# A residual block with conditional rows in fp32 on one core: another order of the first products, and half of the row-block loads issued by ScalarE

## The chip, the core and the metric

One core of a Trainium2 chip runs the kernel. The metric is device microseconds (us) of the program, from its start to its end, as the median of several executions. The hardware profile comes from one execution.

## The reference

The output is `x + relu(concat(x, mean(x), cond, cond) · W + b)` in fp32, with x of four batch rows by 1024 by 512. Cut to what is computed:

```
hidden   = concat([cond, cond], -1)                       # (4, 512)
x_mean   = mean(x, axis=1, keepdims=True)
fused    = concat([x, x_mean, hidden], -1)                # last axis 1536
relation = relu(einsum('bld,do->blo', fused, W) + b)      # W is (1536, 512)
out      = x + relation
```

Only the first 512 rows of W meet every row of x. The mean and the condition give one vector of 512 per batch row, which the kernel works out once for each and adds as a bias.

## The kernel before, in words

**The products.** x has 4096 rows, cut into 32 tiles t of 128 rows. The 512 inputs of a row are cut into four chunks j. TensorE multiplies in a rounded fp32 form, so both sides are split: hi is the rounded value and lo what is left. For each tile and chunk there are three products, `product(t, j, n)` (L356): n=0 is hi·w_hi, n=1 is lo·w_hi, n=2 is hi·w_lo. That is 32·4·3 = 384 matmuls of 128x512 (L366), twelve of them adding up in one PSUM bank per tile. A task `p8.1` is the three products of tile 8 and chunk 1, and `p0.3.2` is a single one.

**How x gets to TensorE.** TensorE needs x transposed, with the inputs on the partitions. Tiles 0 to 3 come row by row (`X`, L206), are gathered (`y`, L232: a copy into another order) and transposed by TensorE itself (`T`, L261, into the PSUM tiles px, po and acc). From tile 4 on, a unit of four tiles comes as a z tile, in four quarters: `Zu.i` (L177) loads partitions 32i to 32i+31 of the z tile of unit u, 256 KB each in pieces of 512 bytes. There are three z buffers, and units 3 to 9 make 28 quarters. VectorE then transposes a chunk of the unit with a stream transpose (`T`, L263) into px or xT. Each transpose is read twice: ScalarE rounds it to hi and sums it for the mean (`h`, L270), and VectorE or GpSimd subtracts hi to get lo (`l`, L276). The weights come the same way: `W` (L181) loads a chunk, `wh` (L215) makes w_hi and `wl` (L222) makes w_lo.

**The rest.** `M` loads four chunks of the mean's weights, `V` the condition's weights (1 MB), `C` and `B` the condition and b. The tasks ac, t, g, d, to, as, m, f, fa, vh, vl, pb and bc work out the bias of each batch row. `K`, `b`, `r`, `F` and `S` take a finished tile out of its bank, add the bias, clamp it, add x and store it.

**What sets the order.** There is no scheduler. The table `ORDER` (L22 to L50) names the tasks one after another, and the loop at L457 issues them as they stand. Letters behind `@` choose an engine: d is VectorE, a is ScalarE, p is GpSimd. Each engine works through its own instructions strictly in that order. A `dma()` (L147) marked `@a` is issued by ScalarE and all others by SyncE (SP), each engine with its own queue. So `W0@a` and `W1@a` are the only transfers that ScalarE issues before the change. `fill` (L133) is a matmul on zeros ahead of the work.

**Semaphores of the transfers.** The transfers take eight semaphores, DMAHW0 to DMAHW7, in turn, whichever engine issues them. A transfer whose semaphore was used eight transfers earlier is issued only when that earlier one has landed. The engine that issues it stands still until then. In the order rows below, that is what `[waits DMAHW2_49]` behind a DMA says.

Of the kernel before, what the change touches and what calls it, by code (L numbers as in the profile page):

```python
# [19 lines left out]


ORDER = """  # L22
W0@a fill W1@a X0.0 X0.1 W2 fill relu fill W3 fill X0.2 fill Z3.1 fill y0.1@d y0.0@p y0.2@p fill T0.0 wh0r@d Z3.2
T0.1 T0.2 wh0l@d h0.0 fill wl0r@p fill y1.0@d y1.1@a T0.3 l0.0@d fill h0.2 wl0l@p fill h0.1 T1.2 T1.0 p0.0.1 T1.1
wh1@d Z3.3 T1.3 p0.0.0 h1.0 p0.0.2 Z3.0 h1.3 l1.0@d p1.0.2 wl1@p h1.2 l0.1@d p1.0.0 l1.3@d wh2@a p0.1.0 p1.0.1 wh3@d
h1.1 p0.1.1 p0.2.0 h0.3 l0.2@d wl2@p C p1.2.0 l1.1@d p1.3.1 V p0.3.0 p1.1.0 B y3.0@d y2.0@a p1.3.0 p0.2.1 Z4.0
l1.2@d p1.1.1 wl3@d p1.1.2 p0.2.2 T2.2 Z4.2 T2.3 p1.2.1 h2.2 T2.0 T2.1 l2.2@d p0.3.2 Z4.3 h2.0 p1.2.2 p3.2 h2.3
l2.0@d h2.1 l2.3@d p2.0 l2.1@d Z4.1 l0.3@d p2.3 p2.2 T3.0 p3.1 T3.3 h3.0 T3.1 p3.0 h3.3 l3.0@d p2.1 h3.1 l3.3@p t3
p3.3 T3.2 M1 K2@d p1.3.2 l3.1@p M0 p0.3.1 K1@a p4.0 t2 M2 h3.2 p0.1.2 ac0@p p6.0 M3 l3.2@d K0@a p4.3 Z5.2 t0 K3@d
p5.3 t1 Z5.3 ac1@d g0.0 p7.2 p6.2 d0.0 Z5.0 g0.1 p5.2 d0.1 g1.0 p5.0 Z5.1 T4.1 T4.3 p5.1 d1.0 T4.2 p6.3 K5@a Z6.0  # L30
T4.0 as0 p4.2 to0 g1.1 p7.3 Z6.3 h4.1 m0.0 p6.1 g2.0 l4.1@p m0.1 p4.1 Z6.2 h4.2 m0.2 p7.1 K4@a m0.3 h4.3 p7.0 Z6.1
K6@a p8.1 l4.3@p l4.2@d h4.0 X4.1 p10.1 f0 Z7.2 d1.1 p9.1 fa0 Z7.1 p10.3 l4.0@d vh0 d2.0 p8.2 g2.1 vl0 Z7.0 p11.2
K7@a T5.3 d2.1 p11.3 T5.2 h5.3 Z7.3 p8.0 T5.0 l5.3@p T5.1 pb0 p10.0 bc0@a h5.0 p10.2 b1@p h5.1 X1.1 l5.0@d p9.3 X2.0
h5.2 b2@d p9.0 as1 Z8.2 to1 p9.2 r1@a l5.1@p l5.2@d p12.3 r2@a X1.0 m1.0 K9@a p8.3 Z8.0 F1@p T6.3 p11.0 T6.1 h6.3
p12.2 b0@p m1.1 h6.1 p12.0 T6.2 K8@a p12.1 b3@p g3.0 T6.0 p11.1 K10@a m1.2 Z9.3 h6.2 d3.0 p13.1 Z8.3 m1.3 h6.0 p14.0
Z8.1 l6.0@d f1 b4@p p13.3 r0@a l6.2@d p14.1 r3@a T7.2 l6.3@p p15.0 fa1 Z9.2 p13.0 T7.0 vh1 F2@p p15.1 K11@a vl1 X5.0
p13.2 F0@d Z9.0 b6@p p15.2 S1 T7.3 pb1 X5.1 l6.1@p p14.3 bc1@a as2 p14.2 K13 F3@p r6@a p16.0 K12 h7.3 p15.3 K14 h7.2
l7.3@p T7.1 p17.0 b5@d h7.1 p19.3 b9@p h7.0 p17.3 r4@a l7.0@d p19.2 to2 g3.1 l7.2@d F4@p p16.2 r5@a m2.0 p18.3 K15
b8@p S4 p18.2 Z9.1 m2.1 p16.3 X3.1 d3.1 m2.2 p19.0 m2.3 p18.1 F5@p T8.0 p16.1 f2 fa2 p20.3 b11@p S5 T8.3 S2 p17.2
vh2 X3.0 h8.0 vl2 p17.1 F6@p X2.1 h8.3 S3 T8.2 p19.1 l7.1@d b7@p S6 p20.0 X4.0 pb2 S0 p18.0 bc2@a l8.3@p X7.0 h8.2  # L40
p20.2 K17 r7@a p20.1 K16 as3 F7@p p22.2 T8.1 l8.0@d p21.3 h8.1 T9.0 S7 r8@a p21.1 l8.1@p X6.1 K19 r11@a p22.1 r9@a
l8.2@d b10@p p22.0 r14@a K18 p21.2 r13@a T9.1 h9.0 p24.2 F13@p T9.2 h9.1 p24.1 T9.3 h9.2 F8@p F9@d p21.0 r15@a p24.0
r10@a F11@p S8 K20 h9.3 p22.3 S13 K21 r17@a p23.1 X6.0 to3 r21@a p23.0 F10@p m3.0 r18@a p23.3 r20@a m3.1 p26.1
l9.3@p m3.2 p25.0 K22 F21@p p23.2 m3.3 r22@a p26.2 F15@p f3 S21 p24.3 S11 r12@a fa3 p27.3 S10 F17@p K23 S15 vh3
p25.1 S9 r16@a vl3 p25.2 r19@a F16@p r23@d p26.0 l9.0@d p25.3 F19@p S16 pb3 X7.1 p26.3 bc3@a S17 F12@p P28 p27.1 K25
p27.2 l9.2@d P30 F18@p p28.2 F14@d r25@a p30.2 l9.1@p K26 p28.0 S14 S18 F25@d P31l p27.0 S19 F23@p r26@a p30.0 K24
S25 p31.2l F26@p S23 K27 p31.0l r24@a S12 p31.1l P29 p31.3l F20@p p30.3 P31r F31l F22@d S31l p29.1 S26 p28.1 S20
r27@d S22 p29.0 F24@d F27@p p28.3 p29.3 F28 S24 p30.1 S27 S28 p29.2 F30 p31.1r F29 S30 p31.0r p31.3r S29 p31.2r F31r
S31r
""".split()  # L50


# [437 lines left out]
```

## Time and profile before

| what | value |
|---|---|
| median of 3 runs | 102.18 us (102.05 to 102.19) |
| span of the profiled execution | 101.1 us |
| TensorE busy, of the span | 95.8 us (95%) |
| VectorE, ScalarE, GpSimd busy | 79.3, 60.6, 80.0 us |
| granted TensorE clock, mean of the core | 0.999 |
| moved by DMA | 27.36 MB, mean 271 GB/s |

The span runs from the first to the last instruction of the profiled execution. The time has about 1.1 us more, which lies around the span. A matmul of 128x512 is shown with 0.39 us though the next starts 0.23 us later, since matmuls are pipelined. In the rows a name such as `lo<-xT,hi` says what is written from what, with the buffers' numbers left out.

### The profile page before, as it was taken

The page shows a single profiled execution, that of the slowest core. Times are in us where ns is not written, and L with a number is a line of the kernel's source. Part 1 is how long each engine was busy: PE and PEld are TensorE (multiplying, and loading weights), DVE is VectorE, ACT ScalarE, POOL GpSimd, SP SyncE. Part 2 cuts the span into 40 slices and gives each one's busy share as a digit, 9 for nine tenths or more (in the row PEclk, how much of TensorE's full clock was granted, in tenths as well). Part 3 has the DMA queues.
Part 4 walks back from the last instruction along what each step waited for, and adds up shares of the span by engine and source line. Part 5 has one row for each costly group of instructions (what it writes and reads, how often), then busy time and mean ns, then how long its engine had stood idle before and what let it go on. Part 6 is the DMA issues. An engine that isn't in the chain of part 4 may idle for free.

```text
span 101.1 us, 1437 instructions
## 1 busy us (share of the span) xinstructions
PE 95.8 (95%) x427; PEld 76.4 (76%) x427; DVE 79.3 (78%) x129; ACT 60.6 (60%) x150; POOL 80.0 (79%) x77
## 2 busy tenths in 40 slices
...
GB/s 46 372 343 227 210 211 316 205 205 322 207 199 191 210 223 197 206 260 298 241 225 209 207 254 307 265 359 408 405 397 400 274 219 345 282 403 328 310 381 161
DMA packets 25345, 27.36 MB, mean 271 GB/s; under 512 B 1397, under 2 KB 15993, under 8 KB 25338
## 3 DMA queue, kind: packets, MB, share of 16 engines
...
q8 instruction: 3, 0.05, 0.2%
...
HBM read 18.88 MB, written 8.39 MB: 270 GB/s over the span
## 4 chain that ended last, share of the span: by engine, by line
PE 38%; DMA 23%; POOL 18%; DVE 10%; ACT 4%; issue 2%; ACTq 1%; SPq 1%; POOLq 0%
PE po L366 37%; DMA z<-in_x_dram 9%; POOL x L455 8%; DMA x<-in_x_dram 8%; DMA x<-in_L_cond_W_dram 6%; POOL lo L276 4%; POOL o L437 4%; DVE acc L320 2%; DVE lo L276 2%; ACT hi L270 2%; DVE w_hi L220 1%; DVE o L446 1%; POOL cond L302 1%; DVE o L441 1%; PE px L261 1%
## 5 line engine op out<-in xcount | busy, mean ns | idle before, releaser
L366 PE MATMUL po<-w_hi,lo 128*128 128x512 f32 (+1 forms) x132 | 50.7, 387 | 0.5 <-DVE lo L276 0.4
L366 PE MATMUL po<-w_hi,hi 128*128 128x512 f32 (+1 forms) x132 | 50.2, 385 | 0.0
L366 PE MATMUL po<-w_lo,hi 128*128 128x512 f32 (+1 forms) x132 | 50.1, 385 | 0.0
L455 POOL TENSOR_TENSOR x<-o,x 128x512 f32<-128x512 f32 x22 | 30.0, 1385 | 0.7 <-DVE o L446 0.4
L366 PEld LDWEIGHTS po<-w_hi,lo 128*128 128x128 f32 x132 | 24.8, 188 | 6.1 <-DVE lo L276 0.8
L366 PEld LDWEIGHTS po<-w_hi,hi 128*128 128x128 f32 x132 | 24.8, 188 | 5.4 <-DVE o L441 0.6
L366 PEld LDWEIGHTS po<-w_lo,hi 128*128 128x128 f32 x132 | 24.7, 188 | 5.0 <-ACT hi L270 0.3
L276 POOL TENSOR_TENSOR lo<-xT,hi 128x512 fp32r<-128x512 f32 x13 | 17.7, 1367 | 9.2 <-ACT hi L270 9.2
L448 ACT ACTIVATE o<-o 128x512 f32<-128x512 f32 x26 | 15.2, 622 | 4.0 <-DVE o L441 3.4
L437 POOL TENSOR_TENSOR o<-o,bias 128x512 f32<-128x512 f32 x10 | 13.9, 1390 | 0.0
L276 DVE TENSOR_TENSOR lo<-px,hi 128x512 fp32r<-128x512 f32 (+2 forms) x20 | 11.5, 588 | 2.2 <-ACT hi L270 2.2
L270 ACT ACTIVATE hi<-px 128x512 fp32r<-128x512 f32 (+2 forms) x20 | 10.3, 517 | 4.8 <-DVE px L263 2.5
L320 DVE SCALAR_TENSOR_TENSOR acc<-w_mean,tot,acc 128x512 f32<-128x512 f32 x16 | 12.0, 748 | 1.4 <-POOL tot L311 1.1
L441 DVE TENSOR_TENSOR o<-po,bias 128x512 f32<-128x512 f32 x16 | 10.5, 679 | 1.6 <-POOL x L455 1.4
L263 DVE STREAM_TRANSPOSE xT<-z 128x512 f32<-128x512 f32 x14 | 9.4, 687 | 2.2 <-POOL cond L302 2.2
L263 DVE STREAM_TRANSPOSE px<-z 128x512 f32<-128x512 f32 x14 | 9.5, 699 | 2.0 <-DMA z<-in_x_dram 1.8
L270 ACT ACTIVATE hi<-xT 128x512 fp32r<-128x512 f32 x14 | 8.7, 624 | 1.8 <-DVE xT L263 1.7
L455 DVE TENSOR_TENSOR x<-o,x 128x512 f32<-128x512 f32 x6 | 7.2, 1194 | 0.0
L298 ACT ACTIVATE term<-wc,cT 128x512 f32<-128x512 f32 x8 | 5.7, 718 | 2.2 <-DVE cT L284 1.4
L433 ACT ACTIVATE o<-po 128x512 f32<-128x512 f32 x10 | 5.9, 590 | 0.8 <-PE po L366 0.8
L302 POOL TENSOR_TENSOR cond<-b_sb,term 128x512 f32<-128x512 f32 x4 | 5.2, 1292 | 1.0 <-ACT term L298 1.0
L224 POOL TENSOR_TENSOR w_lo<-x,w_hi 128x256 fp32r<-128x256 f32 (+1 forms) x4 | 4.2, 1068 | 1.8 <-DVE w_hi L220 1.8
...
## 6 DMA issues: line engine op xcount, KB each, us to landing
out_dram<-x SPq DMA_DIRECT2D x31, 256.0 KB, 3.2
...
z<-in_x_dram SPq DMA_DIRECT2D x28, 256.0 KB, 9.6
x<-in_L_cond_W_dram SPq DMA_DIRECT2D x1, 1024.0 KB, 9.4
w_mean<-in_L_cond_W_dram SPq DMA_DIRECT2D x4, 256.0 KB, 8.2
x<-in_L_cond_W_dram ACTq DMA_DIRECT2D x2, 256.0 KB, 4.6
x<-in_x_dram SPq DMA_DIRECT2D x2, 256.0 KB, 2.8
x<-in_L_cond_W_dram SPq DMA_DIRECT2D x2, 256.0 KB, 5.5
```

The lines of the kernel that those rows point to most:

```text
L263: nc.vector.transpose(xT.rearrange("p (n q e) -> p n q e", q=Q // E, e=E), zs[z_of(u)][:, : n * NQ].rearrange("p n (q j e) -> p n j q e", ...
L270: nc.scalar.activation(his[buf][:, col : col + m], xT, AF.Copy, accum_out=sums[:, r, j, s : s + 1])
L276: nc_of[e].tensor_tensor(los[buf][:, col : col + m], xT, his[buf][:, col : col + m].bitcast(F32), ALU.subtract)
L298: nc.scalar.activation(terms[k], wc[:, k], AF.Copy, scale=cT[:, k, r : r + 1])
L302: nc.gpsimd.tensor_tensor(conds[r % 2], conds[r % 2] if k else b_sb, terms[k], ALU.add)
L320: nc.vector.scalar_tensor_tensor(acc, w_mean[:, j, :], tot[:, r, j : j + 1], acc, ALU.mult, ALU.add)
L366: nc.tensor.matmul(v, lhsT=a[:, col : col + P], rhs=m, start=WAYS[t] != "I" and key not in done, stop=done.count(key) == 3 * J - 1, skip_g ...
L433: nc.scalar.activation(o, bank(t), AF.Copy)
L437: nc_of[e].tensor_tensor(o, o, biases[r], ALU.add)
L441: nc.vector.tensor_tensor(o, bank(t), biases[r], ALU.add)
L448: nc.scalar.activation(o, o, AF.Relu)
L455: nc_of[e].tensor_tensor(x_tile(t), o, x_tile(t), ALU.add)
```

## The change

The code is the same but for the table `ORDER`, which has one line fewer, so every line number after it is smaller by one (L270 becomes L269). The table changes in two ways.

**The first eleven us.** Tile 0 is transposed chunk by chunk in the order 0 to 3, the first product is hi·w_hi (`p0.0.0`) and not lo·w_hi, and tiles 0 and 1 go on together, chunk by chunk. Chunk 3 of w_hi (`wh3`) is made by ScalarE and not by VectorE. All 24 products of tiles 0 and 1 stand before the first of tile 3 (`p3.2`); before, 21 did, and `p1.3.2`, `p0.3.1` and `p0.1.2` came later. Tiles 2 and 3 are transposed in two groups with other work between, not in one. There are 10 fills, not 11.

**The quarters.** Quarters 2 and 3 (partitions 64 to 127) of units 3 to 9 are issued by ScalarE (`@a`): 14 transfers. The quarters of a unit stand together in the order 0, 1, 2, 3. Before, all 28 were issued by SP, mostly spaced out and in orders such as 1, 2, 3, 0 or 0, 2, 3, 1.

The upper part of the diff; the rest of the table changes in the places of Z alone:

```diff
-W0@a fill W1@a X0.0 X0.1 W2 fill relu fill W3 fill X0.2 fill Z3.1 fill y0.1@d y0.0@p y0.2@p fill T0.0 wh0r@d Z3.2
-T0.1 T0.2 wh0l@d h0.0 fill wl0r@p fill y1.0@d y1.1@a T0.3 l0.0@d fill h0.2 wl0l@p fill h0.1 T1.2 T1.0 p0.0.1 T1.1
-wh1@d Z3.3 T1.3 p0.0.0 h1.0 p0.0.2 Z3.0 h1.3 l1.0@d p1.0.2 wl1@p h1.2 l0.1@d p1.0.0 l1.3@d wh2@a p0.1.0 p1.0.1 wh3@d
-h1.1 p0.1.1 p0.2.0 h0.3 l0.2@d wl2@p C p1.2.0 l1.1@d p1.3.1 V p0.3.0 p1.1.0 B y3.0@d y2.0@a p1.3.0 p0.2.1 Z4.0
-l1.2@d p1.1.1 wl3@d p1.1.2 p0.2.2 T2.2 Z4.2 T2.3 p1.2.1 h2.2 T2.0 T2.1 l2.2@d p0.3.2 Z4.3 h2.0 p1.2.2 p3.2 h2.3
-l2.0@d h2.1 l2.3@d p2.0 l2.1@d Z4.1 l0.3@d p2.3 p2.2 T3.0 p3.1 T3.3 h3.0 T3.1 p3.0 h3.3 l3.0@d p2.1 h3.1 l3.3@p t3
-p3.3 T3.2 M1 K2@d p1.3.2 l3.1@p M0 p0.3.1 K1@a p4.0 t2 M2 h3.2 p0.1.2 ac0@p p6.0 M3 l3.2@d K0@a p4.3 Z5.2 t0 K3@d
-p5.3 t1 Z5.3 ac1@d g0.0 p7.2 p6.2 d0.0 Z5.0 g0.1 p5.2 d0.1 g1.0 p5.0 Z5.1 T4.1 T4.3 p5.1 d1.0 T4.2 p6.3 K5@a Z6.0
-T4.0 as0 p4.2 to0 g1.1 p7.3 Z6.3 h4.1 m0.0 p6.1 g2.0 l4.1@p m0.1 p4.1 Z6.2 h4.2 m0.2 p7.1 K4@a m0.3 h4.3 p7.0 Z6.1
-K6@a p8.1 l4.3@p l4.2@d h4.0 X4.1 p10.1 f0 Z7.2 d1.1 p9.1 fa0 Z7.1 p10.3 l4.0@d vh0 d2.0 p8.2 g2.1 vl0 Z7.0 p11.2
-K7@a T5.3 d2.1 p11.3 T5.2 h5.3 Z7.3 p8.0 T5.0 l5.3@p T5.1 pb0 p10.0 bc0@a h5.0 p10.2 b1@p h5.1 X1.1 l5.0@d p9.3 X2.0
-h5.2 b2@d p9.0 as1 Z8.2 to1 p9.2 r1@a l5.1@p l5.2@d p12.3 r2@a X1.0 m1.0 K9@a p8.3 Z8.0 F1@p T6.3 p11.0 T6.1 h6.3
...
+W0@a fill W1@a X0.0 X0.1 W2 fill relu fill W3 fill X0.2 Z3.0 Z3.1 fill fill y0.0@d y0.1@a y0.2@p fill T0.0 T0.1 h0.0
+T0.2 T0.3 wh0r@d h0.1 wh0l@d p0.0.0 wl0r@p l0.0@d h0.2 wl0l@p y1.0@d y1.1@a p0.0.1 h0.3 l0.1@d fill T1.0 T1.1 fill
+T1.2 T1.3 p0.0.2 h1.0 l0.2@d h1.1 l0.3@d p1.0.0 h1.2 l1.0@d p1.0.2 h1.3 wh1@d p1.0.1 fill p0.1.0 wl1@p wh2@a l1.1@d
+p1.1.0 p0.1.1 l1.2@d wh3@a Z3.2@a Z3.3@a C V B Z4.0 Z4.1 p1.1.1 p0.2.0 l1.3@d wl2@d p1.2.0 p0.2.1 wl3@p p1.2.1 p0.1.2
+p1.1.2 p0.3.0 p1.3.0 p0.3.1 p1.3.1 y3.0@d y2.0@a p0.2.2 p1.2.2 T2.2 h2.2 T2.0 h2.0 l2.2@d l2.0@d p0.3.2 p1.3.2 T2.3
+h2.3 T2.1 h2.1 Z4.2@a Z4.3@a l2.3@d l2.1@d p3.2 p2.0 p2.3 p2.2 T3.0 p3.1 T3.3 h3.0 T3.1 p3.0 h3.3 l3.0@d p2.1 h3.1
+l3.3@p t3 p3.3 T3.2 M1 K2@d l3.1@p M0 K1@a p4.0 t2 M2 h3.2 ac0@p p6.0 M3 l3.2@d K0@a Z5.0 Z5.1 Z5.2@a Z5.3@a p4.3 t0
+K3@d p5.3 t1 ac1@d g0.0 p7.2 p6.2 d0.0 g0.1 p5.2 d0.1 g1.0 p5.0 T4.1 T4.3 p5.1 d1.0 T4.2 p6.3 Z6.0 Z6.1 Z6.2@a Z6.3@a
+K5@a T4.0 as0 p4.2 to0 g1.1 p7.3 h4.1 m0.0 p6.1 g2.0 l4.1@p m0.1 p4.1 h4.2 m0.2 p7.1 K4@a m0.3 h4.3 p7.0 K6@a p8.1
+l4.3@p l4.2@d h4.0 X4.1 p10.1 f0 Z7.0 Z7.1 Z7.2@a Z7.3@a d1.1 p9.1 fa0 p10.3 l4.0@d vh0 d2.0 p8.2 g2.1 vl0 p11.2 K7@a
+T5.3 d2.1 p11.3 T5.2 h5.3 p8.0 T5.0 l5.3@p T5.1 pb0 p10.0 bc0@a h5.0 p10.2 b1@p h5.1 X1.1 l5.0@d p9.3 X2.0 h5.2 b2@d
+p9.0 as1 to1 p9.2 r1@a l5.1@p l5.2@d p12.3 r2@a X1.0 m1.0 K9@a Z8.0 Z8.1 Z8.2@a Z8.3@a p8.3 F1@p T6.3 p11.0 T6.1 h6.3
...
```

ScalarE's own order around the loads of units 3 and 4. po, px and xT are what is transposed or evacuated, o_112 the gathered copy of tile 2 (`y2.0`), z_69 the z tile of unit 3 and z_70 that of unit 4. Before:

```order
L218 ACTIVATE w_hi<-x_63 128x512 [waits DMAHW4_49]
L270 ACTIVATE hi_76,sums<-acc 128x128 [waits DVE_49]
L270 ACTIVATE hi_75,sums<-po_140 128x128
L237 ACTIVATE o_112<-x_65 128x512 [waits DMAHW6_49]
L270 ACTIVATE hi_78,sums<-px_142 128x256 [waits PE_49]
L270 ACTIVATE hi_77,sums<-px_141 128x256 [waits PE_49]
L270 ACTIVATE hi_78,sums<-px_142 128x256 [waits DVE_49]
L270 ACTIVATE hi_77,sums<-px_141 128x256 [waits DVE_49]
L270 ACTIVATE hi_79,sums<-px_141 128x512 [waits DVE_49]
```

After:

```order
L217 ACTIVATE w_hi<-x_63 128x512 [waits DMAHW5_49]
L147 DMA z_69<-in_x_dram 32x16x128
L147 DMA z_69<-in_x_dram 32x16x128 [waits DMAHW6_49]
L236 ACTIVATE o_112<-x_65 128x512
L269 ACTIVATE hi_78,sums<-px_142 128x256 [waits PE_49]
L269 ACTIVATE hi_77,sums<-px_141 128x256 [waits PE_49]
L269 ACTIVATE hi_78,sums<-px_142 128x256 [waits DVE_49,PE_49]
L269 ACTIVATE hi_77,sums<-px_141 128x256 [waits DVE_49,PE_49]
L147 DMA z_70<-in_x_dram 32x16x128 [waits DMAHW2_49]
L147 DMA z_70<-in_x_dram 32x16x128 [waits DMAHW6_49]
L269 ACTIVATE hi_79,sums<-px_141 128x512 [waits DVE_49]
```

Four transfers now stand in ScalarE's stream, two ahead of the gathered copy of tile 2 and two ahead of hi_79, the first hi of unit 3. DMAHW6 is the last load of the first rows (`X0.2`) for the first of these waits and Z3.3 for the second. DMAHW2 is `V`.

ScalarE's order around the loads of unit 6 (z_69 again), ahead of hi_84, the first hi of unit 4. Before:

```order
L298 ACTIVATE term_122<-wc,cT 128x512 [waits Pool_49]
L433 ACTIVATE o_108<-po_136 128x512 [waits PE_49]
L315 ACTIVATE acc<-cond_124 128x512 [waits Pool_49]
L298 ACTIVATE term_123<-wc,cT 128x512 [waits Activation_49]
L270 ACTIVATE hi_84,sums<-xT_120 128x512 [waits DVE_49]
```

After, with the two loads ahead of o_108:

```order
L297 ACTIVATE term_122<-wc,cT 128x512 [waits Pool_49]
L147 DMA z_69<-in_x_dram 32x16x128 [waits DMAHW6_49]
L147 DMA z_69<-in_x_dram 32x16x128 [waits DMAHW0_49]
L432 ACTIVATE o_108<-po_136 128x512 [waits PE_49]
L314 ACTIVATE acc<-cond_124 128x512 [waits Pool_49]
L297 ACTIVATE term_123<-wc,cT 128x512 [waits Activation_49]
L269 ACTIVATE hi_84,sums<-xT_120 128x512 [waits DVE_49]
```

ScalarE now passes two loads before it can evacuate o_108 and come to hi_84. SP's order after the change, from the loads of unit 5 (z_71) to those of unit 6 (z_69):

```order
L147 DMA z_71<-in_x_dram 32x16x128 [waits DMAHW5_49]
L147 DMA z_71<-in_x_dram 32x16x128 [waits DMAHW7_49]
L147 DMA z_69<-in_x_dram 32x16x128 [waits DMAHW0_49,DVE_49]
L147 DMA z_69<-in_x_dram 32x16x128 [waits DMAHW2_49]
L147 DMA x_63<-in_x_dram 128x2x512 [waits DMAHW4_49,Pool_49]
```

ScalarE's DMA row that waits for DMAHW0 is Z6.3, and the transfer that used DMAHW0 last is Z6.0, the third of SP's rows. ScalarE comes to Z6.3 only after `Z6.2`, and goes on to o_108 only after Z6.3.

TensorE's order around the transposes of tiles 2 and 3 (o_112 and o_111 into px). Before:

```order
L261 MATMUL px_142<-term_123,o_112 128x128 [waits Activation_49]
L261 MATMUL px_142<-term_123,o_111 128x128 [waits DVE_49]
L261 MATMUL px_142<-term_123,o_112 128x128
L261 MATMUL px_142<-term_123,o_111 128x128
L366 MATMUL po_137<-w_hi,lo_90 128x512 [waits DVE_49]
L261 MATMUL px_141<-term_123,o_112 128x128
L261 MATMUL px_141<-term_123,o_111 128x128
L261 MATMUL px_141<-term_123,o_112 128x128
L261 MATMUL px_141<-term_123,o_111 128x128
L366 MATMUL po_136<-w_lo,hi_75 128x512 [waits DVE_49]
L366 MATMUL po_137<-w_lo,hi_76 128x512
L366 MATMUL po_139<-w_hi,hi_78 128x512 [waits Activation_49]
```

After:

```order
L260 MATMUL px_142<-term_123,o_112 128x128 [waits Activation_49]
L260 MATMUL px_142<-term_123,o_111 128x128 [waits DVE_49]
L260 MATMUL px_141<-term_123,o_112 128x128
L260 MATMUL px_141<-term_123,o_111 128x128
L365 MATMUL po_136<-w_lo,hi_75 128x512 [waits Pool_49]
L365 MATMUL po_137<-w_lo,hi_76 128x512
L260 MATMUL px_142<-term_123,o_112 128x128 [waits DVE_49]
L260 MATMUL px_142<-term_123,o_111 128x128
L260 MATMUL px_141<-term_123,o_112 128x128 [waits DVE_49]
L260 MATMUL px_141<-term_123,o_111 128x128
L365 MATMUL po_139<-w_hi,hi_78 128x512 [waits Activation_49]
```

The second group of four transposes now waits for VectorE, twice: it writes into px beside what l2.2 and l2.0 still read, and stands ahead of the first product of tile 3 (po_139).

## Rows read from the trace of the kernel before

**Rows 1.** The page: the span

```profile
span 101.1 us, 1437 instructions
```

**Rows 2.** Windows: us, busy PE, PEld, DVE, ACT, POOL, clock, DMA share, GB/s

```profile
9.00:13.00 4.00, 3.90 (x21) 3.31 (x22) 2.23 (x8) 1.76 (x7) 1.19 (x1) 1.00 1.22 209
15.00:16.00 1.00, 1.00 (x6) 0.84 (x5) 0.45 (x1) 0.00 (x0) 0.00 (x0) 1.00 1.03 410
28.00:40.00 12.00, 12.00 (x54) 9.94 (x54) 10.56 (x16) 10.19 (x26) 10.41 (x11) 1.00 1.20 206
12.60:94.00 81.40, 81.04 (x361) 66.53 (x360) 70.19 (x106) 54.40 (x127) 72.24 (x63) 1.00 1.09 275
...
15.30:34.60 19.30, 19.30 (x87) 16.00 (x86) 15.51 (x27) 13.83 (x32) 14.24 (x14) 1.00 1.18 231
```

**Rows 3.** Chain of waits, 0 to 12 us: start us, us, what

```profile
1.35 5.58 DMA x<-in_L_cond_W_dram
...
6.95 0.43 DVE w_hi L220
7.38 0.59 DVE lo L276 x3
7.97 1.08 DVE w_hi L220
...
9.10 2.11 PE po L366 x8
```

**Rows 4.** TensorE's timeline: start us, us, instruction, idle before and its releaser

```profile
12.61 0.40 PE L366 MATMUL po<-w_hi,hi 128*128 128x512 f32 x1
...
29.87 0.39 PE L366 MATMUL po<-w_hi,lo 128*128 128x512 f32 x1
...
31.91 0.39 PE L366 MATMUL po<-w_hi,lo 128*128 128x512 f32 x1
...
85.43 0.50 PE L366 MATMUL po<-w_hi,lo 128*128 128x512 f32 x1 [0.36 <-DVE lo L276]
```

**Rows 5.** ScalarE's timeline, 10 to 27 us

```profile
10.09 0.64 ACT L237 ACTIVATE o<-x 128x512 f32<-128x512 f32 x1 [1.51 <-DMA x<-in_x_dram]
...
11.68 0.38 ACT L270 ACTIVATE hi<-px 128x256 fp32r<-128x256 f32 x1 [0.95 <-PE px L261]
...
25.09 0.60 ACT L433 ACTIVATE o<-po 128x512 f32<-128x512 f32 x1 [0.56 <-PE po L366]
```

**Rows 6.** VectorE's timeline, 12 to 18 us

```profile
12.19 0.43 DVE L276 TENSOR_TENSOR lo<-px,hi 128x256 fp32r<-128x256 f32 x1 [0.87 <-ACT hi L270]
...
15.55 0.73 DVE L263 STREAM_TRANSPOSE px<-z 128x512 f32<-128x512 f32 x1 [1.11 <-DMA z<-in_x_dram]
...
17.37 0.65 DVE L276 TENSOR_TENSOR lo<-px,hi 128x512 fp32r<-128x512 f32 x1
```

**Rows 7.** GpSimd's timeline, 27 to 32 us: l4.1 and l4.3

```profile
27.51 1.29 POOL L276 TENSOR_TENSOR lo<-xT,hi 128x512 fp32r<-128x512 f32 x1 [0.37 <-ACT hi L270]
29.79 1.30 POOL L276 TENSOR_TENSOR lo<-xT,hi 128x512 fp32r<-128x512 f32 x1 [0.99 <-ACT hi L270]
```

**Rows 8.** SP's timeline: issues of Z3.0, V and Z6.0

```profile
6.95 0.31 SPq L148 DMA_DIRECT2D z<-in_x_dram  x1
...
9.36 0.40 SPq L148 DMA_DIRECT2D x<-in_L_cond_W_dram  x1
...
24.59 2.93 SPq L148 DMA_DIRECT2D z<-in_x_dram  x1
```

**Rows 9.** DMA issues by window (Z3.0, V, Z6.0): KB, us to landing

```profile
z<-in_x_dram SPq DMA_DIRECT2D x1, 256.0 KB, 8.4
...
x<-in_L_cond_W_dram SPq DMA_DIRECT2D x1, 1024.0 KB, 9.4
...
z<-in_x_dram SPq DMA_DIRECT2D x1, 256.0 KB, 10.0
```

**Rows 10.** Window at the end of the span

```profile
100.70:101.10 0.40, 0.00 (x0) 0.00 (x0) 0.00 (x0) 0.00 (x0) 0.00 (x0) 0.60 0.00 0
```

More of the change, by code (lines that the diff above doesn't have):

```diff
@@ L33 @@
-K7@a T5.3 d2.1 p11.3 T5.2 h5.3 Z7.3 p8.0 T5.0 l5.3@p T5.1 pb0 p10.0 bc0@a h5.0 p10.2 b1@p h5.1 X1.1 l5.0@d p9.3 X2.0
-h5.2 b2@d p9.0 as1 Z8.2 to1 p9.2 r1@a l5.1@p l5.2@d p12.3 r2@a X1.0 m1.0 K9@a p8.3 Z8.0 F1@p T6.3 p11.0 T6.1 h6.3
-p12.2 b0@p m1.1 h6.1 p12.0 T6.2 K8@a p12.1 b3@p g3.0 T6.0 p11.1 K10@a m1.2 Z9.3 h6.2 d3.0 p13.1 Z8.3 m1.3 h6.0 p14.0
-Z8.1 l6.0@d f1 b4@p p13.3 r0@a l6.2@d p14.1 r3@a T7.2 l6.3@p p15.0 fa1 Z9.2 p13.0 T7.0 vh1 F2@p p15.1 K11@a vl1 X5.0
-p13.2 F0@d Z9.0 b6@p p15.2 S1 T7.3 pb1 X5.1 l6.1@p p14.3 bc1@a as2 p14.2 K13 F3@p r6@a p16.0 K12 h7.3 p15.3 K14 h7.2
@@ L38 @@
-l7.3@p T7.1 p17.0 b5@d h7.1 p19.3 b9@p h7.0 p17.3 r4@a l7.0@d p19.2 to2 g3.1 l7.2@d F4@p p16.2 r5@a m2.0 p18.3 K15
[L39 to L47, printed above, removed]
@@ L48 @@
-r27@d S22 p29.0 F24@d F27@p p28.3 p29.3 F28 S24 p30.1 S27 S28 p29.2 F30 p31.1r F29 S30 p31.0r p31.3r S29 p31.2r F31r
-S31r
+W0@a fill W1@a X0.0 X0.1 W2 fill relu fill W3 fill X0.2 Z3.0 Z3.1 fill fill y0.0@d y0.1@a y0.2@p fill T0.0 T0.1 h0.0
+T0.2 T0.3 wh0r@d h0.1 wh0l@d p0.0.0 wl0r@p l0.0@d h0.2 wl0l@p y1.0@d y1.1@a p0.0.1 h0.3 l0.1@d fill T1.0 T1.1 fill
+T1.2 T1.3 p0.0.2 h1.0 l0.2@d h1.1 l0.3@d p1.0.0 h1.2 l1.0@d p1.0.2 h1.3 wh1@d p1.0.1 fill p0.1.0 wl1@p wh2@a l1.1@d
+p1.1.0 p0.1.1 l1.2@d wh3@a Z3.2@a Z3.3@a C V B Z4.0 Z4.1 p1.1.1 p0.2.0 l1.3@d wl2@d p1.2.0 p0.2.1 wl3@p p1.2.1 p0.1.2
```

14 lines of the change are left out of this document (added).

## The prediction

> **What bounds the kernel now.** I read the windows first, then the chain of waits, then the timelines of the engines around the places where the change adds a wait. The profiled execution spans 101.1 us [rows 1] and the median of the runs is 102.18, so I add my sum to 102.18 and let the 1.1 us around the span stand. From 12.6 to 94.0 TensorE is busy 81.04 of 81.40 us at full granted clock [rows 2]. So after the start there is nothing to win but the one gap of 0.36 us at 85.43 [rows 4], and anything that makes TensorE wait for over a moment is lost. Before 12 us the chain runs through the load of a weight chunk, w_hi and lo on VectorE, and then products [rows 3]. The reader is to see two more things. Where the quarters flow alone, the transfers move 206 to 209 GB/s at a full DMA share, and where full-width loads flow, 410 [rows 2]. And of hi and lo for unit 4, l4.1 on GpSimd ends at 28.80 [rows 7], while TensorE takes it at 29.87 [rows 4]: a slack of 1.07 us.
>
> **The first eleven us (A).** TensorE's state is comparable at the first product of tile 3, p3.2. Before, it starts at 12.61 [rows 4] with three products of tiles 0 and 1 still owed. They take 3·0.23 = 0.68 us, so the state "24 products done" is reached at 13.29. After, the limit is the transposes of tiles 2 and 3. The gathered copy y2.0 starts at 10.09, when the last rows have landed [rows 5], and now stands behind two DMA issues, of which the second waits for that same landing. With an issue of 0.4 us, that of V [rows 8], and a copy of 0.64, T2.2 can start at about 11.1. Behind it comes a chain that was not there: hi 0.38 [rows 5], lo 0.43 [rows 6], the second group of transposes, which waits for that lo because it writes into the same bank, and a second hi and lo. Before, the first transposes stood at 11.04 to 11.7 and the first lo at 12.19 [rows 6]. After, the second group starts at about 12.6 and takes 0.6, and p3.2 follows at about 13.2. The gain is **0.1 us**. At best the order saves 0.6 (the cast of w_hi of 1.08 us in the chain [rows 3], against 0.43 for the one ahead of it), at worst the bank chain costs 0.2.
>
> **ScalarE held for unit 4's loads (B).** ScalarE's rows Z4.2 and Z4.3 wait for V and for Z3.3 and stand ahead of hi_79, the first hi of unit 3. The trace before has no such wait. When do V and Z3.3 land? Before, the last quarter of unit 3 was issued at 6.95 and landed 8.4 us later, at 15.35 [rows 8, 9], just ahead of the transpose that waited for it [rows 6], and V landed at 9.36 + 9.4 = 18.8 [rows 8, 9]. The same bytes now flow in two queues side by side. The earliest is 15.3 as before, the latest 18.8; I take the middle, **17.0**. From the landing to the end of l3.0 it takes 17.37 + 0.65 − 15.35 = 2.67 us [rows 6, 9], so l3.0 is ready at 19.7. TensorE comes to p4.0 after the 24 products of tiles 2 and 3, at 13.2 + 24·0.2275 = 18.7, and wants lo one product later, at 18.9. That is **0.8 us** of stall. The bounds are 0 (15.3) and 2.6 (18.8).
>
> **ScalarE held for unit 6's loads (C).** This is the large term. Z6.3 waits for DMAHW0, that is for Z6.0 to land. Behind it on ScalarE stand the evacuation o_108, acc, term and hi_84, and behind hi_84 stand l4.1 on GpSimd and tile 8 on TensorE. Before, the evacuation started at 25.09 [rows 5], while Z6.0 was issued at 24.59 and landed 10.0 us later, at 34.6 [rows 8, 9]. After 17.0, unit 4, the mean's weights, unit 5 and Z6.0 are still to land: 13 transfers of 262 kB, 3.41 MB. At the pace of the stretch before, 231 GB/s [rows 2], the queues would need until 31.8; at the pace of full-width loads, 410, until 25.3. The two halves side by side are nearest to neither, so I take 300, about the middle, and 28.4. With an issue of 0.4 ScalarE goes on at 28.8, **3.7 us** later than at 25.09. l4.1 then ends at 32.5. TensorE wants it at 29.87 − 0.1 + 0.8 = 30.6, which is 1.95 of stall. l4.3, which ended at 31.09 [rows 7] and was due at 31.91 [rows 4], ends at 34.8 against 34.6: 0.2 more. Together **2.15 us**, with bounds of 0 (410 GB/s) and some 6.7 (landing at 34.6 as before). Units 5 to 9 have the same pairs, but their waits are on transfers issued well before, with more finished units between ScalarE and TensorE.
>
> The Trainium skill speaks against the premise of the change. Its page "DMA: Bandwidth & Descriptors", section "Rules for kernel authors", says that two transfers to disjoint partition halves serialize and that spreading transfers over engines does not help bandwidth. By that rule the pace would stay at 206 to 231 GB/s as in [rows 2], and the time would be that of the first rival below.
>
> **The issues themselves (D).** 14 issues at 0.4 us [rows 8] are 5.6 us on ScalarE, which is idle some 27 of the 81.4 us in the long stretch [rows 2]. From 28 to 40 us it is busy 10.19 of 12 [rows 2], and four issues fall there. I take **0.2 us** (0 to 3, below). The wh3 moved from VectorE to ScalarE falls before 10 us, in ScalarE's idle time of 1.51 [rows 5], and is covered. SP loses 14 issues; nothing waits for SP there but transfers that were early.
>
> **Given back (E).** If TensorE runs 2 to 3 us later from 31 us on, VectorE and GpSimd gain that lead, and the gap at 85.43 goes: **−0.4 us** with small ones (0 to −0.5).
>
> **Sum.** −0.1 + 0.8 + 2.15 + 0.2 − 0.4 = +2.65, so 102.18 + 2.65 = **104.8 us**.
>
> **Rivals.**
>
> *The two queues bring no pace (rival 1).* The rows for it are the full DMA share of 1.18 to 1.22 [rows 2]: the 16 engines look busy already. Against it speaks that the same share goes with 410 GB/s when all partitions are written, so that the engines may be waiting for the partitions' side. Then V and Z3.3 land at about 18.4, B is 2.2, Z6.0 lands at 34.6 as before, ScalarE goes on at 35.0, 9.9 late. l4.1 ends at 38.7 against 32.0, a stall of 6.7. In all −0.1 + 2.2 + 6.7 + 0.2 = +9, **111 us**, and more if TensorE's clock falls while it stands: the granted clock is 0.60 in the last window, 3.5 us after the last product [rows 10]. Chance 0.25.
>
> *The halves really flow side by side (rival 2, not slower).* If quarters 0 and 1 leave the other half's side idle, two queues move 400 GB/s and not 206, as 410 in [rows 2] may say. It decides from the point where Z6.0 lands by 25.8 (25.09 + 1.07 − 0.4): C is then covered by the slack of 1.07. Z3.3 lands at 15.3 and B is 0. What is left is A and D: 102.18 − 0.1 − 0.4 + 0.2, **101.9 us**, at best 101.5 with all of A. The Trainium skill, page "SBUF — State Buffer", section "Door 1: The DMA port swizzle", says that partitions 0 to 63 and 64 to 127 are written through separate ports, half of the rate each. The rows of 209 and 410 agree with it; no run here shows two halves at once. Chance 0.15.
>
> *The issues on ScalarE are long (rival 3).* SP's issues under load took up to 2.93 us [rows 8]. If ScalarE's take 1.3 more each, some two in the stretch of unit 6 add 2 us to C, **107 us**. Chance 0.12.
>
> **How the numbers follow.** The forecast has 0.48. A measurement of this kernel can tell some 0.2 us, 0.2%, from no change. Faster by more than that is most of rival 2, 0.11; within it lies 0.05; slower is the forecast, rivals 1 and 3: 0.84. The range reaches from 101.8, rival 2 without its luckiest cases, to 111.0, the middle of rival 1.
>
> **What would show it.** In the profile after, ScalarE should stand idle at 13 to 17 us and at 25 to 28.8, each time ending in a DMA issue; GpSimd's l4.1 should wait for hi until after 30, and TensorE should have gaps near 18.9 and 30.6 that the profile puts down to lo. A pace near 300 GB/s from 17 to 28 us confirms the size of C; 230 there means rival 1, 400 rival 2. ScalarE's DMA issues of over 1 us mean rival 3. The forecast is wrong if TensorE is gapless from 13 to 40 us, or if its gaps lie where no hi or lo of units 3 or 4 is awaited.

## The result and the profile after

The changed kernel takes **111.92 us** (median of 4, 110.43 to 112.84) against 102.19 us, a ratio of 1.085 (95% interval 1.078 to 1.093). Ratios here and below are formed from each kernel's faster executions alone (those within 1.5% of its fastest), so they are smaller than the quotients of the medians. The forecast was 104.8 with a range up to 111.0: the sign was right, the size was not. The execution in the profile, the slowest of the four, spans 110.7 us against 101.1 [rows 1]. The page's span and the granted clock in 40 slices, where it stood at 9 throughout before:

```profile
span 110.7 us, 1439 instructions
...
PEclk9999999976999999999999999999999999999996
```

The chain that ended before reached its last 62 products at 85.43 [rows 4]; now they start at 95.11, 9.7 us later. TensorE's timeline of the changed kernel (start, us, instruction, idle before and its releaser) shows where:

```profile
13.45 0.80 PE L260 MATMUL px<-term,o 128*128 128x128 f32 x4 [0.34 <-DVE lo L275]
14.01 0.47 PE L365 MATMUL po<-w_hi,hi 128*128 128x512 f32 x1
...
23.18 0.56 PE L365 MATMUL po<-w_hi,hi 128*128 128x512 f32 x1 [3.44 <-ACT hi L269]
24.20 0.80 PE L365 MATMUL po<-w_hi,lo 128*128 128x512 f32 x1 [0.47 <-DVE lo L275]
...
25.22 0.63 PE L365 MATMUL po<-w_hi,hi 128*128 128x512 f32 x1
25.65 0.63 PE L365 MATMUL po<-w_hi,lo 128*128 128x512 f32 x1
...
38.62 0.50 PE L365 MATMUL po<-w_hi,lo 128*128 128x512 f32 x1
...
43.83 0.50 PE L343 MATMUL acc<-v_acc,ones 128*128 128x512 f32 x1 [1.75 <-DVE v_acc L339]
```

p3.2 starts at 14.01, against 13.29 on the same count of products before: 0.7 us. p4.0, the first product of unit 3, waits for hi until 23.18, and its second product for lo until 24.20: starts that would be 0.23 apart stand 3.83, 1.02 and 0.60 apart, 4.8 us in all. The products behind it start 0.43 apart and not 0.23, which is 1.0 us over five of them. The windows show the clock: granted 0.76 from 24 to 30 us (0.53 from 25 to 27, 1.00 again from 27), half speed for part of it, after TensorE had stood.

```profile
18.00:24.00 6.00, 2.29 (x9) 1.31 (x7) 2.33 (x4) 1.56 (x5) 0.19 (x1) 0.96 1.13 250
24.00:30.00 6.00, 5.80 (x20) 4.64 (x21) 4.25 (x10) 3.46 (x9) 4.91 (x5) 0.76 1.22 224
```

Around 30 us, where the forecast had its largest term, there is no gap. At 43.83 the matmul that turns the mean into a bias comes 2.1 us after the product before it, a loss of 1.9. What is left, some 1.2 us, lies in small gaps behind 58 us. ScalarE and VectorE in the changed kernel:

```profile
10.69 0.32 ACTq L147 DMA_DIRECT2D z<-in_x_dram  x1
11.05 0.63 ACT L236 ACTIVATE o<-x 128x512 f32<-128x512 f32 x1 [2.07 <-DMA x<-in_x_dram]
...
17.37 4.43 ACTq L147 DMA_DIRECT2D z<-in_x_dram  x2
22.43 0.60 ACT L269 ACTIVATE hi<-px 128x512 fp32r<-128x512 f32 x1 [7.67 <-DVE px L262]
...
32.58 0.60 ACT L432 ACTIVATE o<-po 128x512 f32<-128x512 f32 x1 [1.93 <-DMA z<-in_x_dram]
...
42.10 0.32 ACTq L147 DMA_DIRECT2D z<-in_x_dram  x1
42.47 0.59 ACT L335 ACTIVATE v_acc<-acc 64x512 fp32r<-64x512 f32 x1 [3.58 <-DMA z<-in_x_dram]
```

```profile
21.67 0.73 DVE L262 STREAM_TRANSPOSE px<-z 128x512 f32<-128x512 f32 x1 [6.45 <-DMA z<-in_x_dram]
```

Z3.3 is issued at 10.69, when the first rows have landed, and its window says 10.8 us to landing: 21.5, where the last quarter of unit 3 before landed at 15.35 [rows 8, 9]. VectorE stands 6.45 us for it. Z3.2, issued at 7.88, landed no sooner than 18.9: ScalarE's queue (q10) moved no packet from 7.9 to 12.0 us, and from 12.0 to 13.5 us only these, while SP's (q1) was full:

```profile
q1 hardware_dynamic: 143, 0.54, 99.4%
q10 hardware_dynamic: 4, 0.00, 0.5%
```

So a transfer that a second queue issues late can stand behind what the first one already holds. ScalarE's own standing was not the cause here: Z4.3 was out at 21.80, and ScalarE's first hi still waited for VectorE's transpose until 22.43. The evacuation o_108 starts at 32.58, not at 25.09 [rows 5]. And v_acc, behind the load Z7.3, stands 3.58 us; the chain of waits puts it down to one transfer of SP's, Z7.0:

```profile
32.67 9.42 DMA z<-in_x_dram
42.08 0.02 issue
42.10 0.32 ACTq L147
42.42 0.05 issue
42.47 0.60 ACT v_acc L335
```

### The profile page after: what moved, and what is told of

It reads as the page before. It is cut to its first block, busy times and chain, and to the rows that moved or that the text cites. A ratio compares the mean times of both kernels' runs of the same rounds, so it can differ in the third digit from the quotient of the medians.

```text
span 110.7 us, 1439 instructions
## 1 busy us (share of the span) xinstructions
PE 99.3 (90%) x426; PEld 76.9 (69%) x426; DVE 78.3 (71%) x128; ACT 61.2 (55%) x152; POOL 80.1 (72%) x76
## 3 DMA queue, kind: packets, MB, share of 16 engines
q10 hardware_dynamic: 7680, 4.20, 18.8%
## 4 chain that ended last, share of the span: by engine, by line
POOL 34%; DMA 31%; DVE 12%; PE 11%; issue 4%; ACT 2%; SPq 2%; ACTq 0%; DVEq 0%; POOLq 0%
DMA z<-in_x_dram 24%; POOL o L436 11%; PE po L365 11%; POOL x L454 10%; POOL lo L275 8%; DMA x<-in_x_dram 7%; DVE px L262 2%; POOL cond L301 2%; DVE acc L319 2%; SPq L147 2%; DVE xT L262 2%; DVE lo L275 2%; DVE o L445 1%; DVE o L440 1%; ACT v_acc L335 1%
## 5 line engine op out<-in xcount | busy, mean ns | idle before, releaser
L365 PE MATMUL po<-w_hi,hi 128*128 128x512 f32 (+1 forms) x132 | 51.6, 395 | 3.4 <-ACT hi L269 3.4
L365 PE MATMUL po<-w_hi,lo 128*128 128x512 f32 (+1 forms) x132 | 51.4, 393 | 0.9 <-DVE lo L275 0.9
L365 PE MATMUL po<-w_lo,hi 128*128 128x512 f32 (+1 forms) x132 | 50.8, 389 | 0.0
L365 PEld LDWEIGHTS po<-w_hi,lo 128*128 128x128 f32 x132 | 25.3, 192 | 7.2 <-DVE lo L275 2.1
L269 ACT ACTIVATE hi<-px 128x512 fp32r<-128x512 f32 (+2 forms) x20 | 10.3, 517 | 9.9 <-DVE px L262 7.9
L269 ACT ACTIVATE hi<-xT 128x512 fp32r<-128x512 f32 x14 | 8.7, 624 | 1.4 <-DVE xT L262 1.3
L301 POOL TENSOR_TENSOR cond<-cond,term 128x512 f32<-128x512 f32 x4 | 5.2, 1296 | 2.8 <-ACT term L297 2.8
L454 DVE TENSOR_TENSOR x<-o,x 128x512 f32<-128x512 f32 x6 | 6.2, 1038 | 0.0
```

What stands on the lines that cost most here:

```text
L269: nc.scalar.activation(his[buf][:, col : col + m], xT, AF.Copy, accum_out=sums[:, r, j, s : s + 1])
L301: nc.gpsimd.tensor_tensor(conds[r % 2], conds[r % 2] if k else b_sb, terms[k], ALU.add)
L365: nc.tensor.matmul(v, lhsT=a[:, col : col + P], rhs=m, start=WAYS[t] != "I" and key not in done, stop=done.count(key) == 3 * J - 1, skip_g ...
L454: nc_of[e].tensor_tensor(x_tile(t), o, x_tile(t), ALU.add)
```

## The experiments

The times scattered more in these runs (the kernel before: 101.8 to 106.6 us), so ratios stand with their 95% intervals; where there is none, the time alone decides little and the trace is read. "All on SP" names the changed table without any `@a` at a quarter.

**All quarters on SP.**

```diff
-Z3.2@a Z3.3@a
+Z3.2 Z3.3
...
```

> The changed order with all quarters back on SP (in the changed order's places). Theory 1, that the loss comes from where ScalarE's 14 loads stand in its stream: only the early order is left. p3.2 started at 14.01 in the changed kernel against 13.29 on the same count before, of which some 0.4 us is the load ahead of y2.0; expect p3.2 at 13.5 to 13.7 and 102.3 to 102.9 us, no TensorE gap over 0.5 us after 14 us. Theory 2, that the order of the quarters or the early order costs most of it: 105 us or more.

Measured: 103.0 us, ratio 1.0036 (0.9994 to 1.0077). The same kernel again:

> The kernel with the changed early order and all quarters on SP once more, to narrow its ratio to the kernel before (1.0036, 0.9994 to 1.0077, in the first runs). If the early order is worth what TensorE's last product showed (0.36 us earlier): 0.995 to 0.998. If it is worth nothing: 0.999 to 1.003.

Measured: 103.0 us (102.4 to 105.8), ratio 1.0015 (0.996 to 1.0069). In the first of the two runs p3.2 starts at 13.49, and up to 60 us no gap of over 0.3 us follows:

```profile
12.93 0.81 PE L260 MATMUL px<-term,o 128*128 128x128 f32 x4 [0.34 <-DVE lo L275]
13.49 0.48 PE L365 MATMUL po<-w_hi,hi 128*128 128x512 f32 x1
```

So the early order costs and wins nothing that can be measured, and the whole loss comes with the loads on ScalarE. Theory 2 falls.

Of the 0.7 us at p3.2 all on SP keeps 0.2 (13.49; 13.34 in the second run). The other 0.5 is there as early as 7 us, long before y2.0: the first products start 0.43 to 0.56 us apart in the changed kernel, 0.23 to 0.31 all on SP, though neither waits for anything there. The changed kernel, then all on SP:

```profile
5.46 0.63 PE L365 MATMUL po<-w_hi,lo 128*128 128x512 f32 x1
...
6.95 0.48 PE L365 MATMUL po<-w_lo,hi 128*128 128x512 f32 x1
```

```profile
5.38 0.40 PE L365 MATMUL po<-w_hi,lo 128*128 128x512 f32 x1
...
6.42 0.48 PE L365 MATMUL po<-w_lo,hi 128*128 128x512 f32 x1
```

Profiles of the kernel before and of other versions show such a slow start too. Why it differs between executions stays open, and so does what the early order is worth at equal pace.

**The old order, with nothing but the queue changed.**

```diff
-Z3.2
+Z3.2@a
...
```

> The order of before with nothing but quarters 2 and 3 marked for ScalarE's queue, each in its old place. Theory 1 (place in ScalarE's stream): Z3.2 and Z3.3 stand early, so unit 3 lands by 16 us and most of the loss is gone; 102.5 to 106 us, what is left being holds of ScalarE at units 5 to 7. Rival (two queues by themselves slow the loads down): unit 3 lands after 18 us and the time is over 108 us.

Measured: 108.7 us, ratio 1.047 (1.030 to 1.063). The time and unit 3's landing meet the rival's figures, not theory 1's, but the four executions took 106.1 to 110.0 us, and theory 1's premise, an early Z3.3, did not come about, so the run does not decide between the two. Z3.2 went out at 2.1 us, but Z3.3 only at 8.38, since it had to wait for a weight chunk to land, and landed at 21.3. In this order TensorE also lost 1.72 us at 9.2, 1.30 at 14.2 and 1.94 at 57.5, besides 1.0 at unit 3. At 28 to 32 us both queues carry quarters, and here the pace can be read (row of the two queues: packets, MB, share). The queue-only kernel, then all on SP:

```profile
DMA packets 1618, 0.82 MB, mean 205 GB/s; under 512 B 47, under 2 KB 1616, under 8 KB 1617
...
q1 hardware_dynamic: 973, 0.48, 76.2%
q10 hardware_dynamic: 644, 0.32, 43.8%
```

```profile
DMA packets 1747, 0.87 MB, mean 217 GB/s; under 512 B 53, under 2 KB 1747, under 8 KB 1747
```

Two queues side by side moved 205 GB/s, one queue 217: one window each, and no gain.

**Unit 3 back on SP, or issued early by ScalarE.**

```diff
-Z3.2@a Z3.3@a
+Z3.2 Z3.3
```

> The changed kernel with Z3.2 and Z3.3 alone back on SP. Theory 1: unit 3 lands at 15 to 16 us, the gap of 3.6 us at 19.4 and the slow clock behind it go (5.8 us together), but the lead that covered ScalarE's hold at unit 6 goes too, so a part comes back near 28 to 31 us: 105 to 109 us. Rival (the gaps are independent): the whole 5.8 us is won, 106 us with no new gap between 26 and 38 us.

Measured: 108.6 us (107.2 to 109.7). Unit 3 had landed by 14.7 us and its gap is gone, but ScalarE stood 4.7 us at Z5.3, and later at Z8.3. TensorE lost 0.85 us behind the product at 29.8 and 2.97 behind that at 44.6:

```profile
23.99 1.34 ACT L297 ACTIVATE term<-wc,cT 128x512 f32<-128x512 f32 x2 [4.71 <-DMA z<-in_x_dram]
...
41.35 4.56 ACTq L147 DMA_DIRECT2D z<-in_x_dram  x2
```

A gain of 5.8 us at one place is about 3.3 us at the end: the gaps cover one another. With the pair moved up behind the first loads instead:

```diff
-X0.2 Z3.0 Z3.1
+X0.2 Z3.2@a Z3.3@a Z3.0 Z3.1
```

> The changed kernel with Z3.2 and Z3.3 still issued by ScalarE but right behind its two weight loads. Theory 1 (late issue, behind V): they are issued by 5 us, unit 3 lands by 16.5 us, and the time is that of the run with these two on SP within 1 us. Rival (ScalarE's queue is served later or slower whatever the issue time): Z3.3 lands after 18 us and the gap before unit 3 stays over 1.5 us.

Measured: 115.3 us, ratio 1.119 (1.100 to 1.139), a miss. Z3.3 landed at 15.7, so the rival falls, but unit 3's last quarter, on SP, only at 17.6, and the time is not theory 1's. The two queues took turns from the start: from 4 to 8 us SP's queue moved 0.65 MB and ScalarE's 0.48, against 1.16 and 0.25 all on SP. The first rows (`X0.2`) landed at 13.3, later than in the runs without an early load on ScalarE (9.2 to 12.4). Here an early load on a second queue took its bytes from what the first one carried. The larger loss came later: ScalarE stood 9.0 us at unit 5's loads, TensorE 5.8 us at 38.4, and its clock was at half speed (0.50 granted) from 38 to 42 us.

**Units 3, 6 and 7 back on SP.**

```diff
-Z3.2@a Z3.3@a
+Z3.2 Z3.3
...
-Z6.2@a Z6.3@a
+Z6.2 Z6.3
...
-Z7.2@a Z7.3@a
+Z7.2 Z7.3
```

> The changed kernel with units 3, 6 and 7 on SP, so that ScalarE issues quarters 2 and 3 of units 4, 5, 8 and 9 alone. With only unit 3 on SP, two gaps were left, 0.85 us at 29.8 and 2.97 us at 44.6 with 1.6 us of slow clock behind it. Theory 1 (each gap is a hold of ScalarE at one unit's loads, here units 6 and 7): both gaps go, 102.5 to 104 us. Rival (two queues at work slow all transfers): gaps over 1 us stay before 50 us, 106 us or more.

Measured: 107.2 us, ratio 1.045 (1.038 to 1.052), not the 102.5 to 104 expected. The time is in the rival's range, its gaps of over 1 us before 50 us are not there: ScalarE stood at Z5.3 and at Z9.3, loads that I had thought free, and each stand is followed by TensorE's next gaps (0.95 and 0.85 at 31.0 and 32.4; 1.54 at 54.2).

```profile
25.61 1.34 ACT L297 ACTIVATE term<-wc,cT 128x512 f32<-128x512 f32 x2 [4.86 <-DMA z<-in_x_dram]
...
51.17 0.59 ACT L327 ACTIVATE fold<-acc 64x512 f32<-64x512 f32 x1 [3.53 <-DMA z<-in_x_dram]
```

**Units 6 and 7 later in ScalarE's stream.**

```diff
-Z6.2@a Z6.3@a K5@a
+K5@a
...
-l4.2@d h4.0 X4.1
+l4.2@d h4.0 Z6.2@a Z6.3@a X4.1
...
-p10.1 f0 Z7.0 Z7.1 Z7.2@a Z7.3@a d1.1
+p10.1 f0 Z7.0 Z7.1 d1.1
...
-X2.0 h5.2 b2@d
+X2.0 h5.2 Z7.2@a Z7.3@a b2@d
```

Unit 3 is on SP here too.

> Unit 3 on SP; the loads of units 6 and 7 stay on ScalarE but stand later in its stream, unit 6's behind h4.0 and unit 7's behind h5.2. Theory 1 (the hold costs, not the queue): ScalarE waits under 1 us in all ahead of them, no TensorE gap over 1 us before 45 us, 102.5 to 104.5 us. Rival (late loads cost as much as held ones): the gap moves to the first transposes of units 6 and 7, behind 45 us, and the time stays above 106 us.

Measured: 110.7 us, ratio 1.080 (1.074 to 1.085), a miss. The moved loads themselves did as theory 1 has it: unit 6's pair went out at 32.0 and 32.4 without a stand, unit 7's held ScalarE for 1.03 us. The loss came at loads that had not been moved, unit 5's (4.89 us) and unit 9's (2.90), and p3.2 was 1.7 us later than all on SP, in part since the rows landed late. Taking the holds from two units left those at the others.

**V later.**

```diff
-C V B Z4.0 Z4.1
+C B Z4.0 Z4.1 V
```

> The changed kernel with V (1 MB) behind Z4.0 and Z4.1 in SP's order, nothing else moved. Theory: Z3.3 landed at 21.5 because it was issued at 10.7 into transfers that already held V; without V ahead (1.05 MB at some 390 GB/s is 2.7 us) it lands at 18 to 19.5, the gap before unit 3 shrinks from 3.6 to about 1 us and the slow clock goes; the time falls to 107 to 110 us, less than the gap's 5.8 us because the holds at units 6 and 7 are no longer covered. Rival (the order of V does not matter, the second queue is served late anyway): Z3.3 lands after 20.5 and the time stays at 111 us or more.

Measured: 112.0 us (108.7 to 113.3), above the 107 to 110 expected. Z3.3, issued at 11.97, landed 7.9 us later and not 10.8, at 19.8, and the gap ahead of p4.0 fell to 0.80: V ahead of it had been a part of the delay, and the rival's landing is refuted. Now the hold at unit 6 shows, as the forecast's C had it:

```profile
33.45 0.60 ACT L432 ACTIVATE o<-po 128x512 f32<-128x512 f32 x1 [3.11 <-DMA z<-in_x_dram]
```

```profile
35.84 0.50 PE L365 MATMUL po<-w_hi,hi 128*128 128x512 f32 x1 [2.04 <-ACT hi L269]
37.20 0.80 PE L365 MATMUL po<-w_hi,lo 128*128 128x512 f32 x1 [0.86 <-POOL lo L275]
```

**Unit 7 on SP.**

```diff
-Z7.2@a Z7.3@a
+Z7.2 Z7.3
```

> The changed kernel with unit 7's quarters 2 and 3 alone back on SP. Theory (the gap of 2.24 us at 41.7 is ScalarE held at Z7.3 until Z7.0 has landed, with v_acc behind it): that gap goes and nothing else changes before it; 109.2 to 110.3 us. Rival (the next load on ScalarE takes its place): a gap of over 1.5 us between 42 and 60 us and 111 us or more.

Measured: 113.2 us (107.1 to 114.9). The gap at 43.83 is gone, but the gap ahead of p4.0 was longer in this run (4.14 us), and TensorE stands 1.50 us at 59.3, ahead of the same kind of matmul, after ScalarE had stood 4.00 us at Z9.3. So unit 7's loads had made the gap at 43.83, and the next hold came in its place, as the rival has it; the time, with this scatter, says nothing clear.

**A hold without a second queue.** All on SP, and one read of one element:

```diff
+    @task("hold")
+    def _(e):
+        nc.scalar.activation(one[:1], zs[z_of(5)][:1, 0, :1], AF.Copy)
...
-Z5.3@a p4.3
+Z5.3 hold p4.3
```

> All quarters on SP, and at the place where Z5.3 stood in ScalarE's stream a one-element read of the z tile that waits for Z5.0 to land (26.8 us in the run with all on SP): a hold without a second queue. It ends some 1.5 us after the hold that cost 2.6 us of TensorE by 33 us in the run with units 4, 5, 8 and 9 on ScalarE. Theory (the hold is the cost): TensorE loses 3.5 to 4.5 us between 29 and 38 us, 106 to 107.5 us. Rival (the second queue is the cost): no gap over 0.5 us there and 102.3 to 103.2 us.

Measured: 110.9 us, ratio 1.078 (1.071 to 1.085). The rival falls: one long stand of ScalarE can cost as much as the whole change, with no second queue. It is longer than any stand in the changed kernel (1.93 and 3.58 us), so it does not say that the change's loss is made of stands; most of that is unit 3's late landing. The cost was more than expected because Z5.0 landed at 28.9, not at 26.8, and because TensorE's clock fell behind the gap (0.55 granted from 36 to 42 us; lines are greater by up to four here).

```profile
29.02 0.20 ACT L167 ACTIVATE one<-z 1x1 f32<-1x1 f32 x1 [8.87 <-DMA z<-in_x_dram]
```

```profile
34.46 0.68 PE L369 MATMUL po<-w_hi,hi 128*128 128x512 f32 x1 [4.60 <-ACT hi L273]
```

**A second queue without a hold.** Unit 4's pair alone on ScalarE, then unit 5's pair alone:

```diff
-Z4.2 Z4.3
+Z4.2@a Z4.3@a
```

```diff
-Z5.2 Z5.3
+Z5.2@a Z5.3@a
```

> The changed early order, all quarters on SP but Z4.2 and Z4.3, which ScalarE issues in its idle time between 13.5 and 16 us. Theory (the hold costs, the second queue does not): ScalarE issues both by 15 us without standing, no TensorE gap over 0.5 us between 14 and 45 us, and the time is that of the run with all on SP within 0.5 us. Rival (a second queue at work costs by itself): TensorE's gaps near 19 or 30 us are over 0.5 us and the time is over 104 us.

> The same with Z5.2 and Z5.3 instead: the same number of loads on ScalarE's queue, but at a place where eight transfers are on their way. Theory (the hold costs): ScalarE stands 3 us or more from about 20 us, until a quarter of unit 4 has landed, and TensorE loses 1 to 3.5 us between 29 and 38 us; 104 to 107 us. Rival (the second queue costs, or nothing does): the same time as with unit 4's two on ScalarE, within 0.5 us.

Measured: 102.7 us, ratio 1.0024 (0.996 to 1.009), and 103.3 us (102.3 to 106.6), 1.0001 (0.993 to 1.007). The first is as expected: both loads went out at once, in ScalarE's idle time, and TensorE shows no gap. The second is a miss of the expectation: with the other quarters on SP, Z5.2 and Z5.3 got semaphores that were free, ScalarE stood 0.2 us and not 3, and the ratio shows no loss. The execution in its profile, the slowest, was 1.4 us behind all on SP before any quarter went to ScalarE (p3.2 at 14.87), and TensorE lost 0.96 us at 35.8. Both say the same: two loads on the second queue, where ScalarE need not stand, cost nothing that the ratios can tell.

**The transposes of tiles 2 and 3 in one group**, all on SP:

```diff
-T2.2 h2.2 T2.0 h2.0 l2.2@d l2.0@d p0.3.2 p1.3.2 T2.3 h2.3 T2.1 h2.1
+T2.2 T2.3 p0.3.2 h2.2 T2.0 T2.1 l2.2@d h2.0 p1.3.2 h2.3 l2.0@d h2.1
```

> All quarters on SP, the changed early order, but the transposes of tiles 2 and 3 in one group as before, so that the second four do not wait for lo. If the second group's wait costs what it showed (a gap of 0.34 us of TensorE before it): p3.2 at 13.1 to 13.2 instead of 13.49, 101.8 to 102.5 us, a ratio of 0.996 to 1.000. Rival (the wait only moves to hi and lo ahead of p3.2): p3.2 at 13.4 or later and no difference from the run with all on SP.

Measured: 105.5 us (102.2 to 111.2), ratio 1.002 (0.994 to 1.010). p3.2 started at 13.18, as expected, but 0.9 us were lost again at 52 us. No version here beats the kernel before.

**Long pieces.** Each quarter in rows of 2 KB:

```diff
-dma(e, out=z[i * Q : (i + 1) * Q, : n * NQ], in_=zv[r, i, :, k0 * NQ : (k0 + n) * NQ, :])
+dma(
+    e, out=z[i * Q : (i + 1) * Q].rearrange("t (c w) d -> t c (w d)", c=4),
+    in_=x[r, (k0 + i) * P : (k0 + i + 1) * P, :].rearrange("(c t) d -> t c d", c=4),
+)
```

> All quarters on SP; each quarter loads the same number of bytes into the same 32 partitions, but other rows of x, in pieces of 2 KB instead of 512 bytes (the values of units 3 to 9 are not the reference's). If half the partitions bound the pace of a quarter: 200 to 225 GB/s in stretches where quarters alone flow, as before. If the short pieces bound it: 350 GB/s or more there, and unit 3 lands by 12.5 us. In both cases the time is within 1 us of the run with all on SP, since TensorE does not wait for these loads there.

Measured: 102.8 us (one run). The pace did not change:

```profile
18.00:22.00 4.00, 4.00 (x19) 3.34 (x18) 3.53 (x8) 1.89 (x5) 3.09 (x3) 1.00 1.08 218
```

So the short pieces do not bound a quarter. What still sets it apart from the loads that move 410 [rows 2] is that it writes 32 partitions and not 128; no run varied that alone.

## Why the prediction was wrong

- **A**, −0.1 forecast (−0.6 to +0.2): 0.7 measured. All on SP it was 0.2 and 0.1. The other 0.5 is the slow pace of the first products in this execution, which the term does not have and which no run ties to the loads. y2.0, which the term counted on, did start late, at 11.05 and not at 10.09 [rows 5], but cost nothing: with unit 4's pair alone on ScalarE it started at 10.34, and p3.2 at 13.31.
- **B**, 0.8 forecast (0 to 2.6): 5.8 measured, clock included. This is the step that failed, the landing time of Z3.3: "The earliest is 15.3 as before, the latest 18.8; I take the middle, 17.0." The upper bound was V's landing before, as if the same bytes were ahead of Z3.3. They were not: V was issued at 7.1 and no longer at 9.4 [rows 8], Z3.3 only at 10.7, once X0.2 had landed, while before, as all on SP, the quarters of unit 3 were out by about 7 us; so it stood behind V and Z4.0 and landed at 21.5. The quarters of this unit do not stand together, as I had written of all: Z3.2 and Z3.3 stand far behind Z3.1. I had the wait that sets the issue in front of me and priced it for y2.0 alone. And ScalarE being held, which the term names, is not what cost: the data came late, and VectorE stood for them. The run with V later shows V's part, the one with unit 3 on SP the whole.
- **C**, 2.15 forecast: 0.1 measured, though ScalarE was held as forecast. ScalarE was held until Z6.0 landed, at 32.2 and not 28.4. But TensorE was 6.6 us late by then, ScalarE 7.5, and the slack of 1.07 [rows 4, 7] covers the difference. Where B shrinks, with V later, C appears with 2.0 + 0.9 us. The two terms do not add: the later hold counts from where the earlier one has left TensorE.
- **The pace.** I took 300 GB/s for two queues. They moved 199 to 241 in windows where both carried quarters and little else, against 194 to 228 for one. The rule that I had cited from the Trainium skill, page "DMA: Bandwidth & Descriptors", section "Rules for kernel authors", agrees with this: no gain that matters.
- **D and units 5 to 9.** ScalarE's issues took 0.3 to 0.5 us, so rival 3 falls. But "their waits are on transfers issued well before" was wrong: Z7.3 held ScalarE for 3.6 us and cost TensorE 1.9, and in the experiments Z5.3, Z8.3 and Z9.3 did the like.
- **E** did not come: the gap of 0.36 [rows 4] is 0.39 now. That holds repeat, so that the other engines gained no lead, would explain it; it is not shown.
- **Rivals.** Rival 1's time (111) is near, and its premise, no gain of pace, held. Its place was wrong: its largest term was the hold at unit 6, and the loss came at unit 3. That its time came near is luck. Rival 2 is excluded by the pace.
